# Two gated cross-attention layers on one core: a fold's subtractions on GpSimd, two pools set behind three others, norms taken block by block, and a scattered store put first

## The chip, the cores and the metric

The kernel runs on one NeuronCore of a Trainium2 chip. The metric is the device time of one execution in microseconds (us). All numbers of this part come from the kernel before the change: three timed runs, and one execution that the hardware profiler recorded.

## What is computed

The input `x` has 8 sequences of 256 rows of 1024 numbers, `ctx` has the same shape, and all of it is float32. Four stages follow one another, and each adds to `x` what it makes of the row-normalized `x`, times a learned gate:

```python
x = x + tanh(g_xattn[0]) * autocorrelation(norm(x), ctx, ctx)     # FFT correlation, top 11 lags, weighted gather
x = x + tanh(g_ffn[0])   * lora_ffn(norm(x), W, b, A, B, gate)    # 1024x1024 weight, one of four LoRA ranks per row
x = x + tanh(g_xattn[1]) * grouped_attention(norm(x), ctx, ctx)   # 32 query heads, 8 key heads, wq wk wv wo
x = x + tanh(g_ffn[1])   * (norm(x) @ Wf + b1)                    # Wf: the last weight, folded from several inputs
```

The last weight `Wf` is `W_base` plus half of a product of an encoder, masked coefficients and a Fourier matrix. It does not depend on `x`, so the kernel folds it once.

## The kernel before, in words

**Tiles and passes.** The batch is worked through in two passes of four sequences (`p` = 0 and 1). In a pass, `x` lies in eight tiles `xt[0..7]` of 128 rows; sequence m has the tiles 2m and 2m+1. Large products use a seven-product scheme on 2x2 blocks (`SEVEN` = 1, 2, 6, 7, 4, 5, 3 is the order of the products), so each of them needs sums of weight blocks beforehand. `add_product` adds each product to the four half tiles of `x` that it concerns, partly on VectorE (`residual`, L371), partly on ScalarE and GpSimd (L257, L258, L263 to L267). Product 5 is the last to touch the second tile of a pair, product 3 is the last to touch the first.

**A pass.** First the autocorrelation runs on TensorE together with a generator, `beside`, that makes keys and values of the context (`keys_values`) and, in pass 0 only, the last weight (`fold_last_layer`). Then come `lora_ffn`, `attention`, and `fourier_ffn`, which holds the last stage and the stores to `out`.

**The fold.** After a small product that makes `dec`, `fold_last_layer` runs over four chunks `c`. A chunk loads two tiles `w1in`, adds four TensorE products to them (L320 and L327, on VectorE), and takes four differences of 128x512 elements (L333 to L336), which write the tiles `w_t12` and `w_t47`. SyncE's queue (SP) then stores the blocks to `w1_d` in HBM (L332, L338), from where `fourier_ffn` loads them. The third difference reads the first, the fourth reads the third. Behind these stores in SP's queue come the eight loads of the first feed-forward weight (L119), whose product 6 needs sums of all four of its blocks (L140).

**Pools.** SBUF is given out as a stack of pools. The pools of the autocorrelation and of the keys open together and close together; what opens next lies on the same addresses from the bottom up, and its tiles wait until the earlier ones there are done with. By the tile shapes, in KB of each partition: `kv1` 13 (12 in pass 1), `kv2` 4, `ac1` 9 (the tables `mats`, `inv`, `inv2`), `acw` 24, `ac2` 37. After them open `at_keep` 2, `f0w` 6 (the LoRA operands `ag` and `bl`) and `f0` about 45 (with `xn`, two buffers of 4 KB, at its bottom). After the attention `f1c` 4 and `f1` 40 open at the bottom.

**The last stage.** `fourier_ffn` takes the norms of both blocks of four tiles ahead of everything (`norm_stats`: L349 to L352). `prepare(t)` normalizes a tile (L356), transposes it on TensorE (L366) and copies it (L367). `project(m, ops)` makes the seven products of a pair (L1127) and then stores the pair: the first tile with a plain DMA on SP (L1136), the second, whose rows are reversed, with an indirect DMA on GpSimd's queue (L1137). Both write the same HBM tensor, and the framework makes a later one wait for an earlier one.

**Order of the work.** Nothing is ordered by hand beyond the order of the program. When the program is built, the framework's scheduler fixes the order of instructions on each engine and queue; the order of the program gives the priority, and an instruction that is ready early may be put ahead. On the chip each engine and queue runs its list in that fixed order.

Of the kernel before, what the change touches and what calls it, by code (L numbers as in the profile page):

```python
# [19 lines left out]
P = 128  # L20
B, S, D = 8, 256, 1024
# [3 lines left out]
TT = BP * S // P  # L25
# [21 lines left out]
def flamingo_kernel(ctx: ExitStack, tc: tile.TileContext, a: dict, out: bass.AP):  # L47
# [228 lines left out]
    def fold_last_layer(groups, pools):  # L276


        fp, ps_kv = pools
        group, wt_group = groups  # L280
        co = big_tile(group, [3, KC, R1], "co")
        mk = fp.tile([P, 3, KC, R1], U8, name="mk")
        for e in range(3):
            nc.sync.dma_start(co[:, e], a["coefs"][e].rearrange("(c p) r -> p c r", p=P))
            nc.sync.dma_start(mk[:, e], a["cmask"][e].rearrange("(c p) r -> p c r", p=P))
        encr = big.tile([R1, D], F32, tag=group, name="encr")
        nc.sync.dma_start(encr, a["encr"])
        both = big_tile(group, [2, KC, R1], "both")
        ws, mf = both[:, 0], both[:, 1]
        for e in range(3):  # L290
            nc.vector.tensor_copy(mf, mk[:, e])
            nc.gpsimd.tensor_mul(co[:, e], co[:, e], mf)
        nc.gpsimd.tensor_add(ws, co[:, 0], co[:, 1])
        nc.gpsimd.tensor_add(ws, ws, co[:, 2])
        yield
        dec = big.tile([R1, D], F32, tag=group, name="dec")
        accs = [ps_kv.tile([P, HALF], F32, tag="kv", name="acc") for _ in range(2)]
        for c in range(KC):
            ft = big_tile(group, [2, HALF], "ft")
            nc.sync.dma_start(ft, a["fourier"][c * P : (c + 1) * P, :])  # L300
            for h in range(2):
                nc.tensor.matmul(
                    accs[h][0:R1, :], ws[:, c, :], ft[:, h, :], start=(c == 0), stop=(c == KC - 1)
                )
            yield
        for h in range(2):
            nc.scalar.activation(
                dec[:, h * HALF : (h + 1) * HALF], accs[h][0:R1, :], AF.Copy, scale=0.5
            )
        for c in range(KH):  # L310
            wt = []
            for k in range(2):
                rows = slice((k * KH + c) * P, (k * KH + c + 1) * P)
                wt.append(big_tile(wt_group, [2, HALF], "w1in"))
                nc.sync.dma_start(wt[k], a["w1"][rows, :])
            for k in range(2):
                rows = slice((k * KH + c) * P, (k * KH + c + 1) * P)
                for h in range(2):
                    acc = ps_kv.tile([P, HALF], F32, tag="kv", name="acc")
                    nc.tensor.matmul(  # L320
                        acc,
                        encr[:, rows],
                        dec[:, h * HALF : (h + 1) * HALF],
                        start=True,
                        stop=True,
                    )
                    nc.vector.tensor_add(wt[k][:, h, :], wt[k][:, h, :], acc)  # L327
                if k == 0:
                    yield
            q = [[wt[k][:, j, :] for j in range(2)] for k in range(2)]  # L330
            t12, t47 = big_tile(group, [2, HALF], "w_t12"), big_tile(group, [2, HALF], "w_t47")
            nc.sync.dma_start(w1_d[0, :, c, :], q[0][0])  # L332
            nc.vector.tensor_sub(t12[:, 0, :], q[0][1], q[0][0])  # L333
            nc.vector.tensor_sub(t47[:, 1, :], q[1][1], q[0][1])
            nc.vector.tensor_sub(t12[:, 1, :], q[1][1], t12[:, 0, :])
            nc.vector.tensor_sub(t47[:, 0, :], t12[:, 1, :], q[1][0])  # L336
            for i, t in ((1, wt[1]), (3, t12), (5, t47)):
                nc.sync.dma_start(w1_d[i : i + 2, :, c, :].rearrange("r p d -> p r d"), t)  # L338
            yield

    def norm_stats(tiles):

        n = len(tiles)
        mv = stats.tile([P, TT, 2], F32, tag="mv", name="mv")
        rstd = stats.tile([P, TT], F32, tag="rstd", name="rstd")
        for i, xt in enumerate(tiles):
            st = stats.tile([P, 2, 6], F32, tag="st", name="st")
            for h in range(2):
                nc.vector.bn_stats(st[:, h, :], xt[:, h * HALF : (h + 1) * HALF])  # L349
            nc.vector.bn_aggr(mv[:, i, :], st.rearrange("p a b -> p (a b)"))  # L350
        nc.scalar.activation(rstd[:, :n], mv[:, :n, 1], AF.Sqrt, bias=eps)
        nc.vector.reciprocal(rstd[:, :n], rstd[:, :n])  # L352
        return mv, rstd
# [736 lines left out]
    def fourier_ffn(p, xt, groups):  # L1090
        with (
            tc.tile_pool(name="f1c", bufs=1, reuse_waits="tile") as w1,
            tc.tile_pool(name="f1", bufs=2, reuse_waits="tile") as w2,
            tc.tile_pool(name="f1_t", bufs=4, space=PSUM) as ps_t,
            tc.tile_pool(name="f1_o", bufs=4, space=PSUM) as ps_o,
        ):
            w = stored_weight(groups, lambda r: w1_d[WEIGHTS.index(r)])

            bias1 = w1.tile([P, D], F32, name="bias1")
            nc.sync.dma_start(bias1, a["b1"].partition_broadcast(P))  # L1100
            nc.vector.tensor_scalar(bias1, bias1, tg_f[1], None, ALU.mult)
            norms = [norm_stats(xt[i * NBT : (i + 1) * NBT]) for i in range(TT // NBT)]

            def prepare(t):
                xn = w2.tile([P, D], F32, tag="xn", name="xn")
                normed(xn, xt[t], *norms[t // NBT], t % NBT)
                xnT = w2.tile([P, KC, P], F32, tag="xnT", name="xnT")
                transposed(xnT, xn, ps_t, "t")
                return xnT

            def left(first, second):
                q = [[s[:, k * KH : (k + 1) * KH, :] for k in range(2)] for s in (first, second)]
                s = [w2.tile([P, KH, P], F32, tag=f"s{i}", name=f"s{i}") for i in (1, 2, 4)]
                return left_operands(nc.vector, q, *s)

            def project(m, ops):
                x = [
                    [xt[m * 2 + i][:, j * HALF : (j + 1) * HALF] for j in range(2)] for i in range(2)
                ]
                part = [w2.tile([P, HALF], F32, tag=f"part{i}", name=f"part{i}") for i in range(2)]  # L1120

                for i in range(2):
                    nc.vector.tensor_add(xt[m * 2 + i], xt[m * 2 + i], bias1)
                for r in SEVEN:
                    po = ps_o.tile([P, HALF], F32, tag="o", name="po")
                    for c in range(KH):
                        nc.tensor.matmul(  # L1127
                            po,
                            ops[r][:, c, :],
                            w[r].chunk(c),  # L1130
                            start=(c == 0),
                            stop=(c == KH - 1),
                        )
                    add_product(r, po, x, tg_f[1], ntg_f[1], part)
                b = p * BP + m
                nc.sync.dma_start(out[b * S : b * S + P, :], xt[m * 2])  # L1136
                nc.gpsimd.indirect_dma_start(  # L1137
                    out,
                    bass.IndirectOffsetOnAxis(ap=rows[:, b : b + 1], axis=0),
                    xt[m * 2 + 1],  # L1140
                    None,
                )

            pending = None
            for m in range(TT // 2):
                got = left(prepare(m * 2), prepare(m * 2 + 1))
                if pending is not None:
                    project(*pending)
                pending = (m, got)
            project(*pending)  # L1150

    for p in range(NPASS):
        ga, gb = ("a", "b") if p % 2 == 0 else ("b", "a")
        xt = [xpool.tile([P, D], F32, tag="x", name="x") for t in range(TT)]
        with (
            tc.tile_pool(name="kv1", bufs=1, reuse_waits="tile") as kw1,
            tc.tile_pool(name="kv2", bufs=2, reuse_waits="tile") as kw2,
            tc.tile_pool(name="ac1", bufs=1, reuse_waits="tile") as c1,
            tc.tile_pool(name="acw", bufs=1, reuse_waits="tile") as aw1,
            tc.tile_pool(name="ac2", bufs=2, reuse_waits="tile") as aw2,  # L1160
            tc.tile_pool(name="ac_dft", bufs=4, space=PSUM) as ps_dft,
            tc.tile_pool(name="ac_cor", bufs=1, space=PSUM) as ps_cor,
            tc.tile_pool(name="ac_out", bufs=1, space=PSUM) as ps_out,
# [193 lines left out]
```

## Time and profile before

| | |
|---|---|
| median of three runs | 3411.98 us (3410.40 to 3413.22) |
| the profiled execution, its own time | 3400.72 us |
| its span, first to last instruction | 3399.0 us, mean TensorE clock 0.989 |
| TensorE (PE) busy | 3319.6 us, 98% |
| VectorE (DVE) busy | 2245.2 us, 66% |
| GpSimd (POOL) busy | 1355.3 us, 40% |
| ScalarE (ACT) busy | 859.5 us, 25% |
| DMA | 431.72 MB, 127 GB/s over the span |

In the lines of a profile PE is TensorE's products, PEld its weight loads, DVE VectorE, ACT ScalarE, POOL GpSimd, SP SyncE, which issues most DMAs. L333 is line 333 of the kernel. In a timeline line the first number is the start in us after the first instruction, the second the duration (of all that the line merges), "x8" the number of instructions, and the bracket tells how long the engine had been idle and what ended that. A float32 product counts as two instructions. A busy TensorE can be one that runs slowly, so its starts are read beside its busy time.

### The profile page before, as it was taken

To read this page: it belongs to the slowest core of one execution; us is meant where nothing else is said; L and a number is where in the kernel's file an instruction comes from. 1 tells how busy PE (TensorE), PEld (TensorE's weight loads), DVE (VectorE), ACT (ScalarE), POOL (GpSimd) and SP (SyncE) were. 2 spreads that over 40 slices of the span, in tenths; PEclk is the share of its full clock that TensorE was granted. 3 is DMA by queue.
4 is the path that set the end of the run, shared out by engine and by line. 5 is a ranking of instruction groups with operands and counts; after the bars stand their busy time and mean duration, and the time that the engine had idled before them with its cause. 6 is when DMAs were issued, how large, how long until landed. Compare 5 with 4: busy or idle time off the path is not lost. (4 is left out here: it accounts for less than half of the span.)

```text
span 3399.0 us, 36938 instructions
## 1 busy us (share of the span) xinstructions
PE 3319.6 (98%) x12784; PEld 2281.0 (67%) x12784; DVE 2245.2 (66%) x4229; ACT 859.5 (25%) x2061; POOL 1355.3 (40%) x1211
## 2 busy tenths in 40 slices
PE   8999999999999999999999999999999999999998
PEld 6676456777667767775467766577767777776754
DVE  7787666877777766665657775566666666666662
ACT  1332111322232322222123321122222323222220
POOL 4655212434443443445345541123443443344432
PEclk9999899999999999999999999999999999999999
DMA  7533625333333333343164333143333333333411
GB/s 273 172 115 117 213 87 176 118 137 133 139 126 129 121 119 120 121 163 103 50 203 153 126 102 131 32 158 123 123 121 121 113 123 115 121 123 122 152 38 50
DMA packets 161864, 431.72 MB, mean 127 GB/s; under 512 B 21476, under 2 KB 56292, under 8 KB 161678
## 3 DMA queue, kind: packets, MB, share of 16 engines
q1 hardware_dynamic: 160526, 425.17, 37.1%
q0 software_dynamic: 1152, 4.19, 0.3%
q8 instruction: 102, 1.67, 0.2%
q14 instruction: 84, 0.69, 0.1%
HBM read 350.66 MB, written 78.64 MB: 126 GB/s over the span
## 5 line engine op out<-in xcount | busy, mean ns | idle before, releaser
L719 POOL TENSOR_TENSOR qT<-rope,rope 128x512 f32<-128x512 f32 x128 | 170.0, 1328 | 866.9 <-DVE rope L718 866.9
L954 PE MATMUL po<-wo,oT 128*128 128x512 f32 x960 | 432.1, 593 | 0.0
L925 PE MATMUL ps_q<-xn,wq 128*128 128x256 f32 x1920 | 428.9, 379 | 0.0
L371 DVE SCALAR_TENSOR_TENSOR x<-po,tg,x 128x512 f32<-128x512 f32 x376 | 269.0, 745 | 201.3 <-PE po L954 70.6
L925 PEld LDWEIGHTS ps_q<-xn,wq 128*128 128x128 f32 x1920 | 364.8, 190 | 50.4 <-PE po L678 0.5
L987 ACT ACTIVATE s<-s,nmx 128x256 f32<-128x256 f32 x512 | 255.9, 500 | 276.5 <-DVE nmx L984 276.0
L982 DVE COPY_PREDICATED s<-keep,ps_s 128x512 f32<-128x512 uint8 x256 | 186.2, 730 | 183.0 <-PE ps_s L973 179.6
L954 PEld LDWEIGHTS po<-wo,oT 128*128 128x128 f32 x960 | 177.4, 190 | 175.6 <-issue 170.5
L954 PE MATMUL po<-wo,oS 128*128 128x512 f32 x640 | 287.7, 592 | 0.3 <-DVE x L371 0.3
L925 PE MATMUL ps_q<-xn_t,wq 128*128 128x256 f32 x1280 | 285.6, 379 | 0.0
L1014 ACT COPY wT<-pt 128x512 f32<-128x512 f32 x256 | 138.2, 590 | 516.3 <-PE pt L1008 516.0
L925 PEld LDWEIGHTS ps_q<-xn_t,wq 128*128 128x128 f32 x1280 | 243.2, 190 | 33.0
L1019 PE MATMUL av<-wT,v 128*128 128x256 f32 x1024 | 247.7, 384 | 3.8 <-ACT wT L1014 3.6
L973 PE MATMUL ps_s<-kT,qT 128*128 128x256 f32 x1024 | 247.9, 379 | 0.0
L1019 PEld LDWEIGHTS av<-wT,v 128*128 128x128 f32 x1024 | 192.5, 191 | 79.2 <-issue 44.0
L996 DVE TENSOR_SCALAR s<-s,tot 128x256 f32<-128x256 f32 x512 | 219.6, 469 | 7.7
L981 POOL MEMSET s<- 128x512 f32 x256 | 129.9, 527 | 222.2 <-PE pt L1008 220.5
L954 PEld LDWEIGHTS po<-wo,oS 128*128 128x128 f32 x640 | 119.0, 190 | 136.6 <-issue 128.9
L973 PEld LDWEIGHTS ps_s<-kT,qT 128*128 128x128 f32 x1024 | 191.6, 190 | 25.3 <-DVE x L371 0.5
L258 POOL TENSOR_TENSOR x<-x,part 128x512 f32<-128x512 f32 x80 | 114.9, 1436 | 213.5 <-ACT part L257 193.6
L984 DVE TENSOR_REDUCE nmx<-s 128x2 f32<-128x512 f32 x256 | 175.0, 685 | 8.3
L716 DVE TENSOR_TENSOR rope<-c,tab_q 128x512 f32<-128x512 f32 x128 | 88.4, 691 | 125.8 <-POOL c L240 119.9
(255 smaller groups left out, 5599.4 us busy)
## 6 DMA issues: line engine op xcount, KB each, us to landing
wq<-in_wq_dram SPq DMA_DIRECT2D x104, 512.0 KB, 3.3
wo<-in_wo_dram SPq DMA_DIRECT2D x104, 512.0 KB, 3.5
wq<-wq_d SPq DMA_DIRECT2D x96, 512.0 KB, 3.2
wo<-wo_d SPq DMA_DIRECT2D x96, 512.0 KB, 3.2
w<-w_d SPq DMA_DIRECT2D x36, 512.0 KB, 4.7
wk<-in_wk_dram SPq DMA_DIRECT2D x26, 512.0 KB, 5.8
wv<-in_wv_dram SPq DMA_DIRECT2D x26, 512.0 KB, 4.4
wk<-wk_d SPq DMA_DIRECT2D x24, 512.0 KB, 4.4
```

Source lines behind the costliest of these rows:

```text
L371: nc.vector.scalar_tensor_tensor(xs, ps, g, xs, ALU.mult, ALU.add)
L719: nc.gpsimd.tensor_add(dst, t0, t1)
L925: nc.tensor.matmul(ps[:, l, :], wops[r][:, l, c, :], xo[r][:, c, :], start=(c == 0), stop=(c == KH - 1),)
L954: nc.tensor.matmul(po, ops[r][:, h, t * P : (t + 1) * P], wops[r][:, h, :], start=(h == 0), stop=(h == 1),)
L973: nc.tensor.matmul(ps[:, t, :], qT[i, n][:, l, t * P : (t + 1) * P], kT[:, n * S : (n + 1) * S], start=True, stop=True,)
L981: nc.gpsimd.memset(s, MASKED)
L982: nc.vector.copy_predicated(s, keep[b], ps)
L984: nc.vector.tensor_reduce(nmx, s, AX.X, ALU.max, negate=True)
L987: nc.scalar.activation(s[:, t, :], s[:, t, :], AF.Exp, bias=nmx[:, t : t + 1], accum_out=tot[:, t : t + 1],)
L996: nc.vector.tensor_scalar(s[:, t, :], s[:, t, :], tot[:, t : t + 1], None, ALU.mult)
L1014: nc.scalar.copy(wT[i], pt)
L1019: nc.tensor.matmul(av[:, i, :], kv[step][1][:, n * 2 + c, :], wT[i][:, c, :], start=(c == 0), stop=(c == 1),)
```

## The change

Four edits:

1. In `fold_last_layer` the four differences of a chunk are computed on GpSimd in place of VectorE (16 instructions in all, in pass 0).
2. In `fourier_ffn` the norms of a block of four tiles are taken in `prepare`, when its first tile comes up, in place of both blocks' ahead of everything (both passes).
3. In `project` the indirect store of the second tile is written ahead of the plain store of the first.
4. The pools `kv1` and `kv2` are opened after `ac1`, `acw` and `ac2`, so they lie above them (both passes).

```diff
@@ fold_last_layer
-            nc.vector.tensor_sub(t12[:, 0, :], q[0][1], q[0][0])
-            nc.vector.tensor_sub(t47[:, 1, :], q[1][1], q[0][1])
-            nc.vector.tensor_sub(t12[:, 1, :], q[1][1], t12[:, 0, :])
-            nc.vector.tensor_sub(t47[:, 0, :], t12[:, 1, :], q[1][0])
+            nc.gpsimd.tensor_sub(t12[:, 0, :], q[0][1], q[0][0])
+            nc.gpsimd.tensor_sub(t47[:, 1, :], q[1][1], q[0][1])
+            nc.gpsimd.tensor_sub(t12[:, 1, :], q[1][1], t12[:, 0, :])
+            nc.gpsimd.tensor_sub(t47[:, 0, :], t12[:, 1, :], q[1][0])
@@ fourier_ffn
-            norms = [norm_stats(xt[i * NBT : (i + 1) * NBT]) for i in range(TT // NBT)]
+            norms = {}
             def prepare(t):
+                if t % NBT == 0:
+                    norms[t // NBT] = norm_stats(xt[t : t + NBT])
                 xn = w2.tile([P, D], F32, tag="xn", name="xn")
@@ project, in fourier_ffn
-                nc.sync.dma_start(out[b * S : b * S + P, :], xt[m * 2])
                 nc.gpsimd.indirect_dma_start(
                     out,
                     bass.IndirectOffsetOnAxis(ap=rows[:, b : b + 1], axis=0),
                     xt[m * 2 + 1],
                     None,
                 )
+                nc.sync.dma_start(out[b * S : b * S + P, :], xt[m * 2])
@@ the loop over passes
-            tc.tile_pool(name="kv1", bufs=1, reuse_waits="tile") as kw1,
-            tc.tile_pool(name="kv2", bufs=2, reuse_waits="tile") as kw2,
             tc.tile_pool(name="ac1", bufs=1, reuse_waits="tile") as c1,
             tc.tile_pool(name="acw", bufs=1, reuse_waits="tile") as aw1,
             tc.tile_pool(name="ac2", bufs=2, reuse_waits="tile") as aw2,
+            tc.tile_pool(name="kv1", bufs=1, reuse_waits="tile") as kw1,
+            tc.tile_pool(name="kv2", bufs=2, reuse_waits="tile") as kw2,
             tc.tile_pool(name="ac_dft", bufs=4, space=PSUM) as ps_dft,
```

## The prediction, as it stood before the result was known

> **What bounds the kernel now.** I read the page first, for the bound.
>
> ```profile
> PE 3319.6 (98%) x12784; PEld 2281.0 (67%) x12784; DVE 2245.2 (66%) x4229; ACT 859.5 (25%) x2061; POOL 1355.3 (40%) x1211
> ```
>
> TensorE is the bound, and no edit takes a product away: the change can only win where TensorE waits or runs slowly. In the timeline of TensorE's products these places lie in four seams: the end of the fold in pass 0, the start of `lora_ffn` in pass 1, the starts of `fourier_ffn`, the end. The table of windows sizes the first three; its columns are the window, its length, then busy us and count of PE, PEld, DVE, ACT, POOL, then granted clock, DMA share and GB/s.
>
> ```profile
> 398.00:417.20 19.20, 15.96 (x22) 5.58 (x20) 13.49 (x27) 0.00 (x0) 0.00 (x0) 0.51 0.71 270
> 417.20:424.75 7.55, 7.06 (x34) 6.87 (x34) 5.50 (x22) 2.90 (x5) 0.00 (x0) 0.50 1.02 329
> 2078.50:2096.00 17.50, 11.33 (x63) 9.81 (x63) 11.39 (x37) 2.52 (x6) 0.00 (x0) 0.80 0.56 176
> 1616.00:1628.00 12.00, 8.06 (x40) 5.54 (x39) 11.43 (x20) 3.79 (x6) 5.47 (x5) 0.86 0.00 0
> 3280.00:3292.00 12.00, 8.45 (x38) 6.38 (x38) 10.41 (x19) 3.92 (x6) 0.00 (x0) 0.72 0.01 2
> ```
>
> In each the clock falls below 1.00: the wait is paid a second time as slow products. Then the waits, by timeline. Start of the last stage, pass 1:
>
> ```profile
> 3281.50 1.28 DVE L349 BATCH_NORM_STATS2 st<-x 128x6 f32<-128x512 f32 x2
> 3282.81 0.76 DVE L356 TENSOR_SCALAR xn<-x,mv,rstd 128x1024 f32<-128x1024 f32 x1
> 3283.71 1.94 PE L366 MATMUL pt<-ident,xn 128*128 128x128 f32 x8 [3.55 <-DVE xn L356]
> ```
>
> The first `xn` needs only block 0's norms, but statistics of block 1 stand before it on VectorE. Start of `lora_ffn`, pass 1:
>
> ```profile
> 2083.94 0.81 DVE L356 TENSOR_SCALAR xn<-x,mv,rstd 128x1024 f32<-128x1024 f32 x1 [3.77 <-DMA v_d<-v]
> 2085.10 0.29 ACT L351 ACTIVATE rstd<-mv,eps 128x2 f32<-128x2 f32 x1 [11.40 <-DVE mv L350]
> 2085.92 3.68 PE L625 MATMUL pa<-ag,xnT 128*128 128x68 f32 x16 [4.61 <-ACT xnT L367]
> ```
>
> The second `xn` buffer lies on `kv2` and waits until the last values are stored; behind it queue VectorE's L350, then ScalarE's L351 and its copy L367, for which TensorE waits. The fold's end, SP's queue, and the kernel's end:
>
> ```profile
> 416.04 1.10 SPq L338 DMA_DIRECT2D w_d<-w_t  x2
> 417.19 5.65 SPq L119 DMA_DIRECT2D w<-in_w_dram  x8
> 3386.59 1.41 DVE L371 SCALAR_TENSOR_TENSOR x<-po,tg,x 128x512 f32<-128x512 f32 x2 [2.62 <-PE po L1127]
> 3390.80 0.33 SPq L1136 DMA_DIRECT2D out_dram<-x  x1
> 3394.21 0.97 POOL L1137 DMA_INDIRECT out_dram<-x,rows  x1 [11.17 <-DMA out_dram<-x]
> ```
>
> The next weight's loads go out right behind the fold's last store; the scattered store waits for the plain one, though its tile is ready 2.8 us earlier (3388.0 against 3390.8).
>
> **What the Trainium skill says.** "GPSIMD Engine Reference", § 3.1: an elementwise operation on two tensors takes about twice VectorE's time; here 1.27 us (L267, 128x512) against 0.69 (L333), 1.84 times. "SBUF — State Buffer", § Who interferes with whom: a VectorE operation with two SBUF inputs and a GpSimd one that reads SBUF block each other for whole instructions. The trace agrees: one GpSimd addition takes 3.94 us and ends 1.1 us after the last of VectorE's additions beside it.
>
> ```profile
> 3294.59 3.94 POOL L258 TENSOR_TENSOR x<-x,part 128x512 f32<-128x512 f32 x1 [19.77 <-DVE xn L356]
> 3295.05 2.35 DVE L1123 TENSOR_TENSOR x<-x,bias 128x1024 f32<-128x1024 f32 x2
> ```
>
> "TensorE: Matmul & The Clock Gate", § Part 1: an idle stretch halves the clock until it has been busy again for some us. Here, after the gap of 3.55 us, eight transposes take 1.94 us, later ones 1.04.
>
> **The change, part by part.**
>
> *Scattered store ahead.* No instruction more or less. The indirect store can start at 3388.0, takes 0.8 us to its start (3393.4 to 3394.2 now) and at least 3.3 to land (its own tile view, 3.3/3.9/6.8), so 3392.1. The plain store now waits for that: 2.6 to land (3394.7) and 1.5 us of closing steps, 3396.2 against 3399.0: **2.8 us** off. Bounds: 4.1 if nothing waits, 2 if the landing is slower. At the end of pass 0 SP stands up to 3 us longer in front of L1136; behind it queue the context loads and the x loads of pass 1 (1726.8 to 1737), whose first user on TensorE comes at 1740.3. I take 0; up to 3 lost.
>
> *Norms by block.* The same instructions, later: the 8 statistics (0.69 each) and 4 aggregates (0.2), with ScalarE's table load (1.28), move behind the first pairs. They are wanted for the transposes at 3314.4; VectorE is busy 52 of the last 121 us, so its idle time hides them. If it didn't, its 6.3 us would come back. Without two statistics and an aggregate (1.5 us) in front, `xn` starts 1.4 to 2 us earlier. The gap of 3.55 us (3.94 in pass 0) shrinks to about 2, and the clock should hold: eight transposes 0.9 us less, two products 2.07 to 1.02, sixteen transposes 2.95 to 1.91, together 3.0; in pass 0 1.7 (1.94 to 1.04, 1.85 to 1.02). So 1.6 + 3.0 and 1.6 + 1.7, of which I take **7 us** for both. Lower end 0 (the order built still puts statistics first), upper 12 (both gaps and all slow products).
>
> *Pools.* No instruction changes. In pass 1 `f0` now lies on `acw` and `ac2`, and `kv2` above it, so the 3.77 us wait goes. What is late next is `ag`: it lies on `ac1`, whose last reader (L532) ends at 2076.8; its load is now issued at 2079.9, behind a store, and lands in 4.9 us at least, 2084.8. Issued at 2077 it lands at 2081.9, and L625 starts some 4 us earlier; with a gap under 3 us the slow L625 (3.68 against 1.90) and transposes (1.92 against 1.04) go too, 2.7. Both: 6.7; if `ag` stays behind the store: 1. I take **5**. In pass 0 `ag` and `bl` were loaded at 371.6 and now wait for the autocorrelation's end (389.5) ahead of SP's mask loads and stores; wanted at 394.9, so 0 to 1 us late: **-1**, with the pass-end waits in it.
>
> *Subtractions.* VectorE loses 16 x 0.69 = 11.0 us, GpSimd gains 16 x 1.27 = 20.3, and GpSimd has nothing else from 382 to 431. VectorE's 11 us are not the gain: at 401.5 fourteen L320 products take 12.45 us, 0.89 each against 0.43 (48.08 us for 112 at the end), so TensorE's halved clock sets the pace there. What counts is when the loads at 417.19 go out, since L669 follows at 424.75 and the DMA share there is 1.02. On GpSimd chunk 0's second difference can start at 392.2 (its last L327 ends); 15 more x 1.27 from there is 411.3, and some 2 to 4 us of blocking by four L356 (0.8) and four L206 to L209 (0.69) make 413 to 415, loads at 413.5 to 415.5. So **3 us**. Upper bound 10: of the 26.75 us from 398 to 424.75 about 11.5 are products at full clock (17 x 0.43 and some 40 short ones at 0.11), 15 are lost; lower -3 (loads at 420: a mean of 1.85 us).
>
> Sum: 2.8 + 7 + 5 - 1 + 3 = 16.8, **17 us**. Against the profiled execution's own 3400.72 that is 3384; its time lies 11 us below the median of 3411.98, so I take the difference over: **3395 us**. All low ends give 2 + 0 + 1 - 4 - 3 = -4, all high ends 4 + 12 + 7 + 0 + 10 = 33.
>
> **Rivals.** (A) As above, 3389 to 3402, chance 0.58. (B) With VectorE free TensorE keeps its clock through L320, and the loads go ahead of some stores: the fold gives 10 in place of 3, 3388. For it: SP issues by a list that may put ready loads first. Against: it did not before. 0.16. (C) The lists built hardly differ at the seams, statistics and `ag` stay where they are: 2.8 + 1 + 1, 3407, no measurable change. For it: in the trace statistics of block 1 (L349 at 3263.6 and 3266.0) already run in gaps, so the builder moves work anyway. 0.15. (D) Slower: the differences on GpSimd set the pace of the fold. Each is chained to the one before, SP's stores stand behind the chain in order, and the eight loads behind the stores. The fold loses as soon as the mean difference is over (417 - 392.2) / 15 = 1.65 us; the rest gives 14, so the kernel is measurably slower once it is over (438 - 392.2) / 15 = 3.05, time 3419 and up. For it: the 3.94 us above; against it: the rows' means of 1.27 to 1.46. With other seams that a new order may open, 0.11.
>
> **How the numbers follow.** A measurement of this kernel tells about 0.2%, 6.8 us, from no change. A and B are faster (0.74), C is the same (0.15), D slower (0.11). The likeliest is A: 3395. Low: B with A's better half, 27 us off, 3385. High: 3409, the middle of C, so that D and the rest of C are left out.
>
> **What would show it.** Right: no wait for `v_d` before L356 in pass 1, and L625 before 2083 less the earlier gains; L366 at the last stage's starts after a gap of about 2 us with a clock near 1.00; L1136 last, span ending about 5.5 us after the last L371 in place of 8.2; L333 to L336 on POOL at 1.3 to 1.8 us, L119 a few us earlier. Wrong: gaps over 3 us at these seams, differences over 2 us, or new gaps among the autocorrelation's products in pass 1, whose order the new addresses may also change.

## The result, and the profile after

The changed kernel takes 3420.21 us in the median of 22 runs (3407.93 to 3426.53), the kernel before 3410.91 in the runs beside it (22 runs, 3403.86 to 3413.39). The ratio is 1.0025, with a 95% interval of 1.0018 to 1.0033: slower by about 9 us, where the prediction had a gain (3395 us, range 3385 to 3409). The profiled execution took 3419.06 us, with a span of 3417.3 against 3399.0 and a mean clock of 0.985 against 0.989. In the code after, the lines below L1101 have moved: L1123 is L1125, L1127 is L1129, L1207 (`ag`) is L1209; the scattered store is L1138, the plain one behind it L1144.

The page's line of busy times, after:

```profile
PE 3334.9 (98%) x12784; PEld 2288.2 (67%) x12784; DVE 2249.2 (66%) x4213; ACT 860.4 (25%) x2061; POOL 1373.1 (40%) x1227
```

The 16 differences have gone from VectorE (4229 to 4213 instructions) to GpSimd (1211 to 1227). TensorE has the same 12784 products and yet is busy 15.3 us longer: part of the loss is products at half clock. The starts of TensorE's products cut the span into stages, worked out from the trace:

| us | before | after | difference |
|---|---|---|---|
| start to the first L320 | 385.6 | 394.1 | +8.5 |
| fold and first `lora_ffn` (first L320 to first L925) | 170.6 | 189.9 | +19.3 |
| attention, pass 0 | 1059.7 | 1059.2 | -0.4 |
| last stage, pass 0 (last L954 to its last product) | 109.0 | 108.5 | -0.5 |
| keys and autocorrelation, pass 1 (to the last L532) | 351.4 | 356.1 | +4.7 |
| start of `lora_ffn`, pass 1 (last L532 to first L669) | 14.8 | 8.3 | -6.5 |
| `lora_ffn` and attention, pass 1 | 1188.5 | 1188.0 | -0.5 |
| last stage, pass 1 | 109.8 | 107.3 | -2.5 |
| last product's start to the end | 9.6 | 5.9 | -3.7 |

The differences are taken before rounding. So the start of `lora_ffn` in pass 1 and the end gave a little more than predicted (6.5 for 5, 3.7 for 2.8), the two last stages less than half (3.0 for 7), and the fold, the way to it and the autocorrelation of pass 1 took more than all that back. The windows after (columns as in the prediction) lie at the places of those before: the fold's end, the first weight's loads, the start of `lora_ffn` in pass 1, the two starts of the last stage.

```profile
402.00:438.98 36.98, 32.63 (x79) 17.33 (x78) 19.55 (x56) 4.74 (x9) 14.89 (x12) 0.51 0.52 189
438.98:462.00 23.02, 15.91 (x42) 7.75 (x42) 6.28 (x6) 1.76 (x3) 5.01 (x4) 0.72 0.77 281
2108.00:2125.50 17.50, 15.30 (x84) 10.62 (x83) 13.73 (x48) 5.23 (x10) 1.27 (x1) 1.00 0.57 171
1643.30:1655.30 12.00, 8.75 (x41) 5.78 (x40) 11.93 (x14) 2.25 (x4) 6.00 (x5) 0.86 0.00 1
3304.10:3316.10 12.00, 9.71 (x43) 6.78 (x42) 11.02 (x18) 2.57 (x5) 0.00 (x0) 0.86 0.01 2
```

The third line, with 0.80 before, now shows the full clock; the last went from 0.72 to 0.86. The first two tell of the fold: 60 us from its middle to the end of its loads, at half clock for most of it. SP's queue and TensorE there, in the timeline after:

```profile
420.23 1.70 SPq L338 DMA_DIRECT2D w_d<-w_t  x2
421.98 0.49 SPq L315 DMA_DIRECT2D w1in<-in_w_dram  x1
...
423.40 0.99 SPq L119 DMA_DIRECT2D w<-in_w_dram  x2
...
437.53 0.17 DVE L352 RECIPROCAL rstd<-rstd 128x2 f32<-128x2 f32 x1 [0.36 <-ACT rstd L351]
437.64 1.29 DVE L327 TENSOR_TENSOR w1in<-w1in,acc 128x512 f32<-128x512 f32 x2
438.96 0.38 SPq L338 DMA_DIRECT2D w_d<-w1in  x1
438.98 5.95 PE L669 MATMUL po<-w,xnT 128*128 128x512 f32 x8 [2.56 <-DVE w1in L327]
441.52 1.70 SPq L338 DMA_DIRECT2D w_d<-w_t  x2
443.28 3.55 SPq L119 DMA_DIRECT2D w<-in_w_dram  x6
...
448.41 6.35 PE L669 MATMUL po<-w,xnT 128*128 128x512 f32 x8 [3.48 <-DMA w<-in_w_dram]
```

Read it upwards. At 448.41 TensorE waits for the first feed-forward weight; six of its eight loads (L119) went out only at 443.28, behind the last chunk's stores (L338); these waited for that chunk's sums (L327 at 437.64); and the sums need the eighth `w1in` tile, whose load (L315) stands in SP's list behind the stores of the third chunk, at 421.98. The median `w1in` load lands after 4.6 us, so by estimate this tile is there at about 427; from then to 437.64 its sums stand behind other work in VectorE's list, the norms of the next stage among it (L352). In the kernel before, L315 went out at 393.53, behind the first chunk's first stores, and all eight L119 followed the last store at 417.19. A third wait of 3.82 us follows at 462.19, for sums of the same weight (L140). The differences themselves are quick: 16 of them on GpSimd, 1.33 us in the mean.

Of the 8.5 us on the way to the fold most went in one piece. VectorE and GpSimd at 122 us, after:

```profile
121.02 1.31 POOL L434 TENSOR_TENSOR odi<-ma,mb 128x512 f32<-128x512 f32 x1
...
121.81 10.65 DVE L584 SCALAR_TENSOR_TENSOR w<-took,ex 128x256 f32<-128x256 f32 x1
...
122.27 1.33 POOL L463 TENSOR_TENSOR qe<-xn 128x512 f32<-128x512 f32 x1
123.50 1.35 POOL L464 TENSOR_TENSOR qo<-xn 128x512 f32<-128x512 f32 x1
...
124.74 2.56 POOL L158 TENSOR_TENSOR wv_s<-wv_s,wv 128x512 f32<-128x512 f32 x2
...
127.20 1.33 POOL L238 TENSOR_TENSOR u<-u,m 128x512 f32<-128x512 f32 x1
128.41 1.33 POOL L240 TENSOR_TENSOR v<-w,m 128x512 f32<-128x512 f32 x1
129.63 2.55 POOL L158 TENSOR_TENSOR wv_s<-wv,wv_s 128x512 f32<-128x512 f32 x2
```

L584 usually takes 0.43 us. Here it takes 10.65: it ends 0.3 us after the last of nine GpSimd instructions that follow one another without a pause. TensorE then stands 6.86 us. Up to the fold the two traces show the same order of instructions on every engine, so no list explains this. An equal wait came in pass 1 (L467, 9.08 us at 1922.79), and is in the +4.7 there.

The end, after, where the scattered store no longer waits and the plain one waits for it:

```profile
3408.64 1.41 DVE L371 SCALAR_TENSOR_TENSOR x<-po,tg,x 128x512 f32<-128x512 f32 x2 [2.62 <-PE po L1129]
3410.32 0.98 POOL L1138 DMA_INDIRECT out_dram<-x,rows  x1 [5.24 <-DVE x L371]
...
3413.70 0.33 SPq L1144 DMA_DIRECT2D out_dram<-x  x1
```

And the start of the last stage in pass 1. Block 0's statistics were over long before, in both kernels. Of block 1's eight, six stood ahead of the first `xn` before and four do now (3288.1, 3290.6, 3303.9 and the one below): the builder still puts ahead what is ready early. The gap is 2.29 us in place of 3.55.

```profile
3304.83 0.69 DVE L349 BATCH_NORM_STATS2 st<-x 128x6 f32<-128x512 f32 x1
...
3306.09 1.53 DVE L356 TENSOR_SCALAR xn<-x,mv,rstd 128x1024 f32<-128x1024 f32 x2
3307.04 3.40 PE L366 MATMUL pt<-ident,xn 128*128 128x128 f32 x16 [2.29 <-DVE xn L356]
```

### The profile page after: what moved, and what is told of

Its sections match the earlier page's. It is cut to its first block, busy times and chain, and to the rows that moved or that the text cites. A ratio compares the mean times of both kernels' runs of the same rounds, so it can differ in the third digit from the quotient of the medians.

```text
span 3417.3 us, 36937 instructions
## 1 busy us (share of the span) xinstructions
PE 3334.9 (98%) x12784; PEld 2288.2 (67%) x12784; DVE 2249.2 (66%) x4213; ACT 860.4 (25%) x2061; POOL 1373.1 (40%) x1227
## 5 line engine op out<-in xcount | busy, mean ns | idle before, releaser
L954 PE MATMUL po<-wo,oT 128*128 128x512 f32 x960 | 432.2, 593 | 0.0
L925 PE MATMUL ps_q<-xn,wq 128*128 128x256 f32 x1920 | 428.9, 379 | 0.0
L371 DVE SCALAR_TENSOR_TENSOR x<-po,tg,x 128x512 f32<-128x512 f32 x376 | 268.9, 745 | 214.4 <-PE po L954 70.3
L925 PEld LDWEIGHTS ps_q<-xn,wq 128*128 128x128 f32 x1920 | 365.2, 190 | 50.1 <-PE po L678 0.5
L954 PEld LDWEIGHTS po<-wo,oT 128*128 128x128 f32 x960 | 177.6, 190 | 175.5 <-issue 170.4
L954 PE MATMUL po<-wo,oS 128*128 128x512 f32 x640 | 287.7, 593 | 0.3 <-DVE x L371 0.3
L925 PE MATMUL ps_q<-xn_t,wq 128*128 128x256 f32 x1280 | 285.6, 379 | 0.0
L925 PEld LDWEIGHTS ps_q<-xn_t,wq 128*128 128x128 f32 x1280 | 243.4, 190 | 32.8
L954 PEld LDWEIGHTS po<-wo,oS 128*128 128x128 f32 x640 | 119.1, 190 | 136.5 <-issue 128.8
L258 POOL TENSOR_TENSOR x<-x,part 128x512 f32<-128x512 f32 x80 | 109.0, 1362 | 190.6 <-ACT part L257 190.6
L984 DVE TENSOR_REDUCE nmx<-s 128x2 f32<-128x512 f32 x256 | 175.0, 685 | 8.3
L263 POOL TENSOR_TENSOR x<-x,part 128x512 f32<-128x512 f32 x80 | 104.1, 1303 | 178.9 <-DVE part L371 178.9
```

The source lines that it names most:

```text
L371: nc.vector.scalar_tensor_tensor(xs, ps, g, xs, ALU.mult, ALU.add)
L925: nc.tensor.matmul(ps[:, l, :], wops[r][:, l, c, :], xo[r][:, c, :], start=(c == 0), stop=(c == KH - 1),)
L954: nc.tensor.matmul(po, ops[r][:, h, t * P : (t + 1) * P], wops[r][:, h, :], start=(h == 0), stop=(h == 1),)
L984: nc.vector.tensor_reduce(nmx, s, AX.X, ALU.max, negate=True)
```

## Experiments

Two theories for the fold. **List theory**: the loss comes from where the builder of the program (the scheduler that fixes every list) put the eighth `w1in` load in SP's list. **GpSimd theory**: the slower, chained differences make it. For the stretches ahead of the folds, the **lock theory**: a VectorE instruction that reads two operands from SBUF can be kept waiting by a whole series of GpSimd instructions, by chance, so that executions differ. Ratios are to the kernel before, run beside each; its median differed from one occasion to another (3406.85 to 3411.25), so ratios are compared, not times. The stage is that of one profile each.

| kernel | median us | ratio, 95% interval | fold stage us |
|---|---|---|---|
| changed | 3420.21 | 1.0025 (1.0018 to 1.0033) | 189.9 |
| subs_only | 3423.54 | 1.0037 (1.0024 to 1.0051) | 187.1 |
| pools_only | 3418.21 | 1.0025 (1.0015 to 1.0034) | 177.0 |
| norms_store | 3403.66 | 0.9983 (0.9976 to 0.9990) | 174.0 |
| no_subs | 3409.01 | 0.9992 (0.9983 to 1.0001) | 182.0 |
| act_before | 3412.51 | 1.0003 (0.9997 to 1.0010) | 175.0 |
| act_after | 3409.41 | 0.9998 (0.9989 to 1.0006) | 176.3 |
| act_nosubs | 3405.80 | 0.9986 (0.9977 to 0.9994) | 173.9 |
| grp_nosubs | 3413.19 | 1.0007 (0.9999 to 1.0014) | 179.6 |
| act_ns | 3398.94 | 0.9977 (0.9968 to 0.9985) | 170.9 |
| wv_old_pools | 3399.73 | 0.9980 (0.9971 to 0.9989) | 175.0 |
| wv_act | 3400.24 | 0.9969 (0.9959 to 0.9980) | 174.1 |
| ke_ns | 3427.20 | 1.0051 (1.0037 to 1.0064) | 174.2 |
| kewv_act | 3421.27 | 1.0029 (1.0018 to 1.0040) | 175.5 |
| before_again | 3412.65, one run | | 174.0 |

### The edits apart

`subs_only` is before with edit 1, `pools_only` before with edit 4, `norms_store` before with edits 2 and 3, `no_subs` the changed kernel without edit 1. Each is part of the diff shown, so none is repeated.

> Before with the GpSimd differences alone. List theory: the loss of 19 us in the fold comes from the place of the eighth w1in load (L315) in SP's queue; here too it stands behind the third chunk's stores, so the fold loses 15 to 19 us and nothing else moves: about 3427, ratio 1.004 to 1.006; L315 last goes out after 415 and the first L669 starts near 440. GpSimd theory: the slower differences themselves make the loss, same 15 to 19 us. Pool theory: the loss of the fold needs the new pools (LoRA loads ahead of the stores); 0 to 3 us here, about 3412. VectorE's stall of 10 us at 121.8 is not expected by the pool theory; the chance theory allows it in any execution.

> Before with the keys' pools above the autocorrelation's, alone. List theory: L315 is behind the third chunk's stores here too, though the differences are on VectorE, so the fold loses 10 to 19 us; the start of lora_ffn in pass 1 gains 6.5; together +4 to +12, about 3419, ratio 1.001 to 1.004. GpSimd theory: the fold is as before, so -6, about 3405, ratio 0.998. Pool theory of the stalls: VectorE stands 10 us in L584 at 121.8 and 7 us in L467 in pass 1 again, which adds 8 to 13 us to either.

> Before with the norms by block and the scattered store ahead, without the differences on GpSimd and without the new pools. All theories: the last stage's starts give 0.6 and 2.6 us, the end 3.7, together 7 us: about 3404, ratio 0.998; fold and autocorrelation as before, first L669 at about 424.8. The prediction's own sum for these two edits was 9.8 us: 3401.

> The changed kernel with the differences back on VectorE. GpSimd theory: the fold's 19 us come back, so -10 against before, about 3400, ratio 0.997. List theory: L315 stays behind the third chunk's stores, so most of the loss stays: about the time of before less 0 to 6, 3405 to 3412, ratio 0.998 to 1.001; the first L669 starts at 435 or later.

The differences alone lose 0.37%, and the new pools alone 0.25%, though these move no instruction to another engine. In both, the eighth load and two of the eight L119 have changed places in SP's list in the same way (minus is before, from the list of `subs_only`):

```
@@ minus: before, plus: subs_only; SP's list, w_d<-... are the fold's stores
 L338 DMACopy w_d<-w1in 128x2x512
-L315 DMACopy w1in<-in_w_dram 128x1024
 L338 DMACopy w_d<-w_t_2779 128x2x512
...
 L338 DMACopy w_d<-w_t_2832 128x2x512
+L315 DMACopy w1in<-in_w_dram 128x1024
 L332 DMACopy w_d<-w1in 128x512
+L119 DMACopy w_2886<-in_w_dram 128x1024
+L119 DMACopy w_2887<-in_w_dram 128x1024
 L338 DMACopy w_d<-w1in 128x2x512
```

That is the list theory's mark. The median of `pools_only` does not decide by itself: with VectorE's waits on top, which were expected to add 8 to 13 us, the GpSimd theory allows times up to 3418 too. Its profile, of its fastest run (3410.28 us) and without such a wait, has the late load, but its fold is only 6.4 us longer than in the first profile of before, where 10 to 19 were expected. `no_subs` says more: the differences are on VectorE again, the load is still late, and the fold takes 182.0 us, so the 19 us did not all come back as the GpSimd theory had it. It comes out level with before, as the list theory had it. But from `no_subs` to the changed kernel, with the load late in both, the ratio rises from 0.9992 to 1.0025: the place of the load is not the whole loss. The late load costs more where the differences are on GpSimd; in the trace VectorE's list then holds the last two L327 back further. `pools_only`:

```profile
414.12 0.50 SPq L315 DMA_DIRECT2D w1in<-in_w_dram  x1
...
423.96 1.28 DVE L327 TENSOR_TENSOR w1in<-w1in,acc 128x512 f32<-128x512 f32 x2
...
428.29 4.30 SPq L119 DMA_DIRECT2D w<-in_w_dram  x6
```

From L315 to L327 it is 9.8 us here and 15.7 in the changed kernel, where more of the next stage's norms and sums stand ahead. From the end of L327 to the first of the six L119 it is 3.05 us here and 4.35 there: about 1.3 us is what the slower differences cost by themselves. `norms_store` is faster by 0.17%, 6.9 us by the medians (3410.52 for before beside it): that part of the change is a gain by itself.

### The eighth load taken out of SP's list

In the three kernels `act_before` (the control), `act_after` (on the changed kernel) and `act_nosubs` (on `no_subs`) one load is issued by ScalarE's queue; in `grp_nosubs`, also on `no_subs`, its tile comes from the other ring of big tiles.

```diff
-                nc.sync.dma_start(wt[k], a["w1"][rows, :])
+                (nc.scalar if c + k == KH else nc.sync).dma_start(wt[k], a["w1"][rows, :])
# grp_nosubs, in place of that:
-                wt.append(big_tile(wt_group, [2, HALF], "w1in"))
+                wt.append(big_tile(group if c + k == KH else wt_group, [2, HALF], "w1in"))
```

> Control: before, with the eighth w1in load issued by ScalarE's queue in place of SP's. The load goes out at about 394 in either, so both theories expect the time of before within 4 us, 3407 to 3414; if the load, waiting at the head of ScalarE's list, holds up the copies L367, 1 to 3 us more.

> The changed kernel with the eighth w1in load on ScalarE's queue: SP has no L315 behind the third chunk's stores and all eight L119 behind the last. List theory: the loss of 19 us in the fold shrinks to 0 to 5, so 3398 to 3406, ratio 0.996 to 0.999; first L669 at 428 or earlier after the same start of L320 as before. GpSimd theory: the slower differences keep 12 us or more of the loss: 3413 or more.

> The changed kernel with the differences on VectorE and the eighth w1in load on ScalarE's queue. List theory: nothing of the fold's loss is left, the other three edits give 7 (norms and store) and 6 (pools): 3398, ratio 0.996. If the pools' loss of 8 us does not come from the load's place in the list but from their addresses: 3409 as without this edit. GpSimd theory has no view of it beyond 3398 to 3409.

> The same as the kernel before it in this list, but the eighth w1in load stays on SP and its tile is taken from the other ring of seven big tiles, so that it need not wait for the first chunk's store. List theory: L315 goes out ahead of the first stores, 3395 to 3400, as for the load on ScalarE's queue. Address theory: 3409.

The control is level with before. In `act_after` the differences are still on GpSimd, and the fold takes 176.3 us in place of 189.9; the ratio falls from 1.0025 to 0.9998, intervals apart. SP's list has its old shape again:

```profile
430.97 2.04 SPq L338 DMA_DIRECT2D w_d<-w_t  x2
433.06 5.27 SPq L119 DMA_DIRECT2D w<-in_w_dram  x8
```

The first L669 starts at 438.65, not by 428 as expected and hardly ahead of the changed kernel's 438.98; but behind it TensorE no longer stands still (23.35 us busy of the 23.35 to 462.00, against 15.91 of 23.02). Four kernels that share the new pools, norms and store show the two causes together:

| fold us, ratio | differences on VectorE | differences on GpSimd |
|---|---|---|
| eighth load early | 173.9, 0.9986 (`act_nosubs`) | 176.3, 0.9998 (`act_after`) |
| eighth load late | 182.0, 0.9992 (`no_subs`) | 189.9, 1.0025 (changed) |

With the differences on GpSimd the load's late place, with all that the builder moves along with it, is worth 13.6 us of the fold and about 9 by the ratios; with them on VectorE it is 8.1 and about 2, the last not clear of noise. The differences cost 7.9 us of the fold and about 11 by the ratios where the load is late, and 2.4 and about 4 where it is early (those two intervals overlap by 0.0005). So the GpSimd theory's 12 us or more did not stay once the load was early; but the two causes are worth more together (16.0 us of the fold) than apart (8.1 and 2.4). The medians of `act_after` stayed above the expected 3398 to 3406, and `act_nosubs` above 3398: both profiles hold a wait of VectorE of 9 us in pass 1. `grp_nosubs` told something else than meant: the builder left the load behind the third chunk's stores (at 420.93), although by the code its tile need not wait for a store of the first chunk, and the fold kept 5.7 us of loss against `act_nosubs`. So a free buffer alone did not bring the load forward, and the loss went with the place in the list.

### VectorE's waits

The profile of before lies 10 us under its median, so it was run once more.

> Before once more, one profiled execution. The first one took 3400.72 us, 10 under the median. Lock theory: a usual execution of before has a wait of VectorE of 7 to 10 us somewhere (L467 at 1900 or L584 at 121), which the first did not have; 3408 to 3413 us. Rival: no such wait, and the time is 3404 or less.

3412.65 us, with this in pass 1, VectorE and GpSimd of `before_again`:

```profile
1902.14 1.27 POOL L462 TENSOR_TENSOR ko<-cn 128x512 f32<-128x512 f32 x1
1902.23 9.06 DVE L467 SCALAR_TENSOR_TENSOR ke<-end,ke 128x512 f32<-128x512 f32 x1 [8.00 <-POOL ke L461]
1903.37 2.49 POOL L158 TENSOR_TENSOR cx_t<-cx,cx_t 128x512 f32<-128x512 f32 x2
1905.82 1.27 POOL L238 TENSOR_TENSOR u<-u,m 128x512 f32<-128x512 f32 x1
1907.05 1.26 POOL L240 TENSOR_TENSOR v<-w,m 128x512 f32<-128x512 f32 x1
1908.27 2.48 POOL L158 TENSOR_TENSOR cx_t<-cx_t,cx 128x512 f32<-128x512 f32 x2
```

The first execution had no such instruction; of the 14 kernels and repeats that keep L467 on VectorE, 9 profiles have it. The stage in pass 1 takes 355.5 to 359.4 us with it and 351.4 to 356.8 without, 3.8 us apart in the mean. The fold of `before_again`, 3.4 us longer than in the first profile, goes with another chance, the moment at which TensorE's clock falls to half. In the first profile of before and in `act_ns` that is 12.8 and 12.4 us after the first L320, and the stage takes 170.6 and 170.9 us; in the eight other profiles with the early load and the differences on VectorE it is 6.8 to 8.6 us after it, and the stage takes 173.9 to 175.5. In the four kernels of the table above it is 7.4 to 8.6, so there this chance is alike. So the profile that I predicted from was a lucky one, and 18 us between the two profiles stand for 9 between the medians.

L584's wait of 10 to 11 us in pass 0 showed in 4 of 6 profiles with the new pools (the changed kernel, `no_subs`, `act_after`, `grp_nosubs`) and in none of 7 with the old ones. It costs 5 to 6 us: the first L320 comes at 393.7 to 394.8 with it and at 388.6 and 388.7 without. Two tries to take the waits away:

```diff
# wv_act, wv_old_pools: sums of the value weights, pass 0
-                eng = Short(nc.gpsimd if kind == "wv" else nc.vector)
+                eng = Short(nc.vector if kind == "wv" else nc.vector)
# ke_ns, kewv_act: L467, with the factor of L500 changed from 2 S to -S
-            nc.vector.scalar_tensor_tensor(ke, end, -2.0, ke, ALU.mult, ALU.add)
+            nc.scalar.activation(end, end, AF.Copy, scale=-2.0); nc.gpsimd.tensor_add(ke, ke, end)
```

> As act_nosubs (norms, store, new pools, eighth load on ScalarE's queue), with the sums of the value weights (L154, L158, pass 0 only) on VectorE in place of GpSimd. Lock theory: the series of nine GpSimd instructions behind L584 at 122 us shrinks to four, so L584 takes at most 5 us, TensorE's gap at 127 is under 2 us and L320 starts at 387 to 390 in every execution; 3401 to 3404 against 3405.8. Rival (L584 waits for something else, or VectorE's 16 further instructions cost as much): L584 takes 10 us again or L320 starts at 392 or later, 3406 or more.

> Both edits of the two kernels ahead of it in this list, on act_nosubs. Lock theory: no VectorE instruction over 6 us, the spread of the runs narrower than the 16 us of act_nosubs, 3397 to 3401. Rival: 3405 as without them.

> Norms by block and scattered store ahead, pools and differences as before, and L467's sum with two SBUF inputs taken off VectorE: ScalarE multiplies end by -2 in place, GpSimd adds it to ke. Lock theory (a VectorE instruction that reads two SBUF operands waits until a series of GpSimd instructions without a pause is over): VectorE shows no instruction of 9 us at 1900 to 1925; without this edit about half of the executions have it and lose 4 us of TensorE, so 3401 to 3403 against 3403.7. Rival: the wait goes to the next VectorE instruction of that kind and the time stays at 3404; GpSimd's 16 more instructions could also cost up to 2 us.

`wv_act` came out as the lock theory has it: L584 takes 0.42 us, L320 starts at 387.9, the 8 runs lie within 5.2 us (the 13 of `act_nosubs` within 16.0), and the ratio is 0.9969. It is no proof: L584 starts there 1.2 us after GpSimd's last instruction has ended, so the two no longer meet, and whether a shorter series makes a shorter wait was not seen. L467's wait is in this profile too, and a gap of 4.66 us at 127, expected to be under 2, came with VectorE's further work. That the long instructions wait for GpSimd's series is thus read from the timing in the traces and argued, not shown by an experiment. The two `ke` kernels are slower. The long L467 is gone, as expected, but pass 1 lost over 20 us elsewhere, TensorE waiting for copies on ScalarE, where the new instruction stands ahead of them: in `ke_ns` a product (L412 at 1799.32) waits 7.04 us for such a copy (L515), which runs right behind the new L467 at 1798.16. So the time that L467's wait is worth was not shown this way. Last, the pools by themselves, with the load on ScalarE's queue in both:

> act_nosubs with the pools as they were: norms by block, scattered store ahead, eighth load on ScalarE's queue. Lock theory: L320 starts at 386 to 387.5, no 10 us in L584; the start of lora_ffn in pass 1 waits 15 us in all again, 5 more than in act_nosubs; together about the same as act_nosubs, 3402 to 3406. Rival (the new pools gain their 5 us net): 3410 or more.

> wv_act with the pools as they were. Lock theory: with these pools L584 does not wait, so moving the value weights' sums to VectorE gives nothing or loses a little against act_ns, 3403 to 3407, 3 to 6 us more than wv_act. Rival (the sums' move is worth 5 us for another reason): 3397 to 3401.

Both medians lie under what was expected, as that of before beside them does (3406.85). `act_ns` is `act_nosubs` with the old pools: 0.9977 against 0.9986, so no net gain of the new pools is shown, though the start of `lora_ffn` in pass 1 takes 14.6 us in the one and 9.9 in the other. `wv_old_pools` is `act_ns` with the sums moved and level with it, so moving the sums brings nothing where L584 does not wait; that its 3399.73 lies in the rival's range means little, since `act_ns` takes 3398.94 without the move. With the sums moved the new pools are at 0.9969 against 0.9980; the lock theory expects this gain, but the intervals overlap, so it is not shown. Five kernels beat both kernels of the case (`norms_store`, `act_nosubs`, `act_ns`, `wv_old_pools`, `wv_act`); `wv_act`, 0.31% faster than before, has the lowest ratio.

## Why the prediction was wrong, point by point

**Scattered store ahead: right, a little small.** 2.8 predicted; the end is shorter by 3.7 us, and by as much in every later kernel with it but `wv_act` (3.3). The span ends 4.5 us after the last L371, not 5.5. At the end of pass 0, from its last product to the first L412 of pass 1, the changed kernel lost nothing (15.4 us in both), and later kernels with this edit lost up to 1.4 us.

**Norms by block: right mechanism, too large.** 7 us predicted for both passes. The last stages take 110.3 and 109.6 us in the mean of five profiles with the old norms, and 108.5 and 107.3 in the changed kernel: 4.1. With the store the two edits were put at 9.8 us, and `norms_store` gained 6.9. The gaps shrank as said (3.55 to 2.29 and, in pass 0, 3.94 to 2.72). The mis-sized term is the clock, which was to hold after a gap of about 2 us: in pass 1, after a gap of 2.29 us, it fell to half all the same, for 3.4 us in place of 6.8 (at the start of `lora_ffn`, where the longest gap is now 1.70 us, it did hold). The first sixteen transposes still take 3.40 us, against 1.91 for a later sixteen, and they now all stand ahead of the first product. Nor did all of block 1's statistics move back: four of the eight did.

**Pools: the seam was right, the rest was not.** At the start of `lora_ffn` in pass 1 I counted 5 and got 6.5, and 4.9 in the mean of the profiles (10.1 us in seven with the new pools, 15.0 in seven with the old, the two kernels with L467 changed left out); the wait for `v_d` is gone and `ag` is next (issued at 2107.45, TensorE waits 1.70 us for it), as the prediction had it. Pass 0 was put at -1. It cost 2 us without any wait (the first L320 at 388.6 against 385.6 to 387.3), and 5 to 6 more in four of six profiles, through L584. The engines' lists there are the same with either order of pools, and GpSimd's instructions on the moved tiles have a median of 1.30 us in place of 1.27, as `act_nosubs` against `act_ns` shows. Why VectorE loses its turn more often with them stays open. I had read the Trainium skill's rule ("SBUF — State Buffer", § Who interferes with whom: a VectorE instruction with two SBUF inputs contends with a GpSimd instruction that reads SBUF, and what they contend for is an exclusive lock) as a wait for one instruction, at most 4 us in my rows. In the traces the wait lasts as long as a series of seven to ten.

**Subtractions: the wrong sign, and the failed step.** The step is "What counts is when the loads at 417.19 go out". True, but its working moved instructions inside a list that it took as given: 15 differences chained from 392.2, loads at 413.5 to 415.5. The builder made other lists. In SP's it put L315 behind the third chunk's stores, and by that six of the eight loads behind the fourth's, at 443.28; in VectorE's it put more of the next stage's work ahead of the last sums. The 3 us to be gained became 19.3 lost between the two profiles: 13.6 by the load's late place, 2.4 by the differences on GpSimd with the load early (near the -3 that I had set as the lower bound, and not clear of noise), and the other 3.3 by the lucky clock of the first profile, since the fold of `act_nosubs` takes 173.9 us against 170.6. Why the builder moved the load is open.

**The rivals.** D had the sign and the time (3419), but not the mechanism: the mean difference took 1.33 us, under its threshold of 1.65. C was right in part: half of block 1's statistics stayed ahead. B came nearest to what happened in the fold, from the other side: loads did move in SP's list, and I had written that SP may put ready loads first. I gave no case to a load that moves back. The prediction's "-4" for all low ends left that out, and so the range was too narrow.

## What to carry to other kernels

Where a program is ordered by a builder, an edit that only changes an engine or an address can move a DMA in a queue, as `subs_only` and `pools_only` show; compare the lists of each queue and engine before pricing the edit, and ask of each load behind which stores it could fall. Two such edits are not worth the sum of their parts, as the table of four kernels shows. One profiled execution may lie well under the median: look for what a usual run has that it lacks before its waits are priced. And a series of GpSimd instructions without a pause is a risk for a VectorE instruction beside it that reads two operands from SBUF: in these profiles two such instructions waited, in some executions and not in others, each time for about what was left of the series.

## What the runs showed that I had not expected

A VectorE instruction of 0.43 us took 10 to 11.5 us in four profiles, and one of 0.69 to 1.8 us took 9.1 in nine; each time it ended 0.3 to 0.6 us after GpSimd's series. In the profile of before L584 started in the same place, 0.4 us ahead of the next GpSimd instruction, and took 0.67 us; then that GpSimd instruction took 1.46 us in place of 1.27. In the changed kernel it started 0.46 us ahead of the next one and lost. Who goes first at such a boundary seems to decide between 0.2 us for one engine and 10 us for the other; what settles it was not found. It differs between executions of one program: of the two profiles of before, with the same order on every engine, one has L467's wait and one has not, and 4.5 of the 12 us between them lie in that stage.
